# A graph-attention layer on one core: 138 instead of 120 groups of edges counted, and eight more looked up, weighed and gathered last

## The chip, the cores and the metric

The kernel runs on one core of one Trainium2 chip. The metric is device microseconds of one execution, the median of three runs. The profile is of one more execution, taken by the hardware profiler. PE is TensorE, DVE VectorE, ACT ScalarE, POOL GpSimd and SP SyncE.

## The reference

A layer of graph attention over 12,500 nodes with 64 features and 400,000 edges with 64 features, a residual and a layernorm. The edges are sorted by destination, and destinations are drawn so that low node numbers have far more edges than high ones.

```python
h_src, h_dst = x[src], x[dst]
e = leaky_relu(concat([h_src, h_dst, edge]) @ W_attn + b_attn)[:, 0]
m = concat([h_src, edge]) @ W_ne
ex = exp(e - segment_max(e, dst)[dst])
alpha = ex / segment_sum(ex, dst)[dst]
z = segment_sum(alpha[:, None] * m, dst)
out = layernorm(x + relu(concat([x, z]) @ W_out))
```

So each edge needs its source's row of `x` twice: its dot product with a part of `W_attn` for the score, and the row itself, weighed by `alpha`, for the sum.

## The kernel before

**Groups.** 512 edges make a group (128 partitions by 4 edges), and there are 782 groups, the last of them a quarter full. A group takes one of two ways.

*Gathered groups* (662, from group 120 on). Four indirect DMAs per group, issued from GpSimd (L335), fetch the source rows with their score's part from a table in HBM into a buffer `zx` of four groups (a "part"); there are nine such buffers (`ZB`). SyncE's queue loads the edge features beside them. `scores` (L366 to L388, VectorE) makes a part's scores; L377 is the instruction that waits for the gathered rows. `softmax` (L664 on) then treats a whole batch at once, in four legs, between which the ends of its rows go through a one-partition line and back by DMA (L599, L605). It begins with a transpose (L694). `weights` (L791) spreads alpha over the destinations' slots, `products` (L808, in the last two batches L812) are the matmuls, and `add_in` (L827) adds them to `acc`.

*Dense groups* (the first 120, whose few destinations have thousands of edges each). They need no gather. First they are *looked up*: ScalarE turns the low seven bits of the source numbers into ones and zeros (`look_turn`, L427 and L428), TensorE multiplies by the table of scores (`look_products`, L438), VectorE picks by the high bits (`look_scores`, L463 to L469), and `look_rows` (L448 on) adds the edges' share. Then whole rounds of dense groups join a batch's softmax in its spare rows. Then they are *counted* (`dense_counts`, L477 to L493): ScalarE makes one tile per edge place of ones at the pair (high bits, destination's place), in buffers called `big`, VectorE makes `lows`, ones at the low bits times alpha (L480), and TensorE multiplies the two into a table source by destination, which `dense_sum` (L503, and L506 for the sixth and seventh destination of a group) adds into `counts`. At the end of a chunk of groups `counts` is multiplied by `x` (L562) and set to zero (L575).

**The order of the work** is written out by hand. Every engine runs its instructions in the order of the code. There are 43 batches: 39 of 16 groups, then 10, 10, 12 and 6. In batch `k` the code first issues the gathers (of parts one to three, the fourth a little later, so GpSimd runs ahead), then does the parts' scores, and between these and the softmax's legs a few dense groups: the next ones to be looked up and the next ones to be counted. `alike` says how many: at most four (before group 84) or three (from there), and never across a round's begin, a change in the number of destinations (`NODS`) or, for counts, a chunk's end. A round is free for counting once its look-ups are done and it has joined a softmax. Counts end in batch 38. Blocks of four times 128 nodes are finished (`finish0` to `finish3`: projection, residual, layernorm, output) as soon as no later edge can reach them; block 0, which holds the dense groups' destinations, in three steps in one of the late batches.

**The tail.** After the last batch's softmax come its weights, its products (L812), the additions (L827), and the last two blocks' matmuls (L1042) and layernorm (L1071 to L1090).

**The head** packs the sources' low bits into rows for the look-ups (`low_rows`), loads the dense groups' lists round by round (`dense_list`, L230) and works out their places.

Of the kernel before, what the change touches and what calls it, by code (L numbers as in the profile page):

```python
# [9 lines left out]
F32 = mybir.dt.float32  # L10
I32 = mybir.dt.int32
# [4 lines left out]
P = 128  # L16
# [11 lines left out]
BIG = 6  # L28
# [7 lines left out]
ROUNDS = (12, 12, 12, 12, 12, 12, 12, 12, 12, 12)  # L36
DB = len(ROUNDS)
EACHS = ((84, 4), (120, 3))
EACH = max(n for _, n in EACHS)
# [19 lines left out]
def sorted_path(ctx, tc, x, dst, idx, edge, w_ne, w_attn, b_attn, w_out, out, flag):  # L59
# [24 lines left out]
    ones_row = const.tile([1, P], F32, name="ones_row")  # L84
    nc.vector.memset(ones_row, 1.0)
# [24 lines left out]
    assert HC * ND == P and HC * D <= 512 and sum(chunk_sizes) == DG == NODS[-1][0]  # L110
# [4 lines left out]
    def each_of(g):  # L115
        return next(n for upto, n in EACHS if g < upto)

# [7 lines left out]
    edges_ = sorted({*begins, *(upto for upto, _ in NODS), *(upto for upto, _ in EACHS)})  # L125
    spans = list(zip(edges_, edges_[1:]))
    DN = DBL * P

# [37 lines left out]
    places = const.tile([P, NB * NOD], I16, name="places")  # L166
    nc.gpsimd.iota(places, pattern=[[1, NB * NOD]], base=0, channel_multiplier=0,
                   allow_small_or_imprecise_dtypes=True)
    s_src = const.tile([P, NB], F32, name="s_src")
    low, place = (const.tile([P, T, DG], F32, name=n) for n in ("low", "place"))  # L170
# [11 lines left out]
    rel = const.tile([1, DG], I32, name="rel")  # L182
# [40 lines left out]
    _, sixth, seventh, probe = cut(pps, 2 * P, NB, NB, 8)  # L223
    more_nodes, w_dst, w_src = (sixth, seventh), sixth[:, 0:D], seventh[:, 0:D]
# [18 lines left out]
    def dense_places(srcs, fit):  # L243

        assert max(n for _, n in NODS) <= FIT + len(more_nodes)
# [7 lines left out]
        nc.scalar.activation(low, parted[1], AF.Copy)  # L253
# [7 lines left out]
        nc.vector.tensor_tensor(place, high, wide(fit[:, 1]), op=OP.mult)  # L261
        nc.vector.tensor_tensor(place, place, slot_, op=OP.subtract)
        for a, b in spans:
            if nodes_of(a) > FIT:
# [24 lines left out]
    def slots_of(k):  # L289

        g0, G = starts[k], sizes[k]
        drel = chunks.tile([P, T, BG], F32, name="drel", bufs=3)
# [69 lines left out]
    def scores(g0, n, zx, drel, b0, plain):  # L362
# [6 lines left out]
        pr = feats.tile([P, SG, T, D], F32, name="pr", bufs=1)  # L369
# [37 lines left out]
    def look_loads(g0, n):  # L407

        many = nodes_of(g0)
        wrow = tiny.tile([P, EACH, NOD], F32, name="wrow_d", bufs=1)[:, :, 0:many]  # L410
        nc.sync.dma_start(out=wrow[:, 0:n], in_=wins[0][g0:g0 + n, 0:many].unsqueeze(0).to_broadcast([P, n, many]))
        return dense_edges(g0, n, "ed", True), wrow
# [28 lines left out]
    def look_rows(g0, n, loads):  # L441
# [4 lines left out]
        pr = feats.tile([P, SG, T, D], F32, name="pr", bufs=1)  # L446
# [12 lines left out]
    def look_scores(g, found):  # L459

        pr = feats.tile([P, SG, T, D], F32, name="pr", bufs=1)
# [9 lines left out]
    def dense_counts(g):  # L471
# [14 lines left out]
        for j in range(nodes_of(g) - FIT):  # L486
            at = wide + j * NB
            hi = big().rearrange("l p t -> l (p t)")[:, 0:T * NB].rearrange("l (t h) -> l t h", t=T)
            for t in range(T):
                nc.scalar.activation(hi[:, t], places[:, at:at + NB], AF.Square, bias=place[:, t, g:g + 1])  # L490
            nc.scalar.activation(hi, hi, AF.Relu, scale=-1.0, bias=1.0)
            for t in range(T):
                nc.tensor.matmul(more_nodes[j], lows[t], hi[:, t], start=(t == 0), stop=(t == T - 1), skip_group_check=True)  # L493
        return g, to

    def dense_sum(g, to):
# [7 lines left out]
        for j in range(nodes_of(g) - FIT):  # L504
            at = counts[:, :, ds(vs[0] + FIT + j, 1)]
            nc.vector.tensor_tensor(at, at, more_nodes[j].unsqueeze(2), op=OP.add)  # L506
# [9 lines left out]
    def dense_weights(g0, n):  # L516

        many = nodes_of(g0)
        w = tiny.tile([P, T * EACH * NOD], F32, name="wd", bufs=1)[:, 0:T * EACH * many]
# [6 lines left out]
        return w  # L526

# [38 lines left out]
    def node_pick(g0, pairs):  # L566

        pr = feats.tile([P, SG, T, D], F32, name="pr", bufs=1)
# [5 lines left out]
        if g0 + chunk_sizes[-1] < DG:  # L574
            nc.vector.memset(counts, 0.0)  # L575
# [55 lines left out]
    def between(k):  # L631
# [13 lines left out]
        mask = rows.tile([P, 2, P], F32, name="mask", bufs=2)  # L645
        nc.scalar.activation(mask, pen, AF.Relu, bias=1.0)
        return step, same, pen, mask

    def at_ends(step, same, pen, mask):
# [6 lines left out]
    def lines_of(step, same, pen, mask):  # L656
# [4 lines left out]
        return step, same, pen, mask, rw  # L661

    def softmax(k, about, carry, d=None, carry_d=None):
# [8 lines left out]
        step, same, pen, mask = about[0:4]  # L672
# [29 lines left out]
        to_lines(ends_of, bnd)  # L702
        yield
        in_lines()
        rw = about[4]
# [158 lines left out]
    ids = pre.tile([DG, P, 2 * T], I32, name="ids", bufs=1)  # L864
    nc.sync.dma_start(out=ids, in_=idx[0:DG])
# [10 lines left out]
    with before:  # L876
# [23 lines left out]
        with tc.manual_schedule(engines={EngineType.DVE, EngineType.Pool, EngineType.Activation, EngineType.PE, EngineType.SP}):  # L900
# [27 lines left out]
            nc.vector.tensor_copy(edge_both, pwt[:, 2, 0:D])  # L928
            d0f = pre.tile([1, NG], F32, name="d0f", bufs=1)
# [7 lines left out]
            relf = pre.tile([1, DG], F32, name="relf", bufs=1)  # L937
# [5 lines left out]
            room = pre.tile([1, DG], F32, name="room", bufs=1)  # L943
            for a, b in spans:
                nc.vector.memset(room[:, a:b], float(ND - nodes_of(a)))
            over_ = pre.tile([1, DG], F32, name="over_", bufs=1)
# [13 lines left out]
            parted_row = pre.tile([DG, P, T], I32, name="parted_row", bufs=1)  # L960
# [867 lines left out]
```

## Time and profile before

| | |
|---|---|
| median of 3 runs | 3384.53 us (3383.27 to 3386.39) |
| the profiled execution | 3384.66 us |
| its span, first to last instruction | 3382.9 us |
| TensorE matmul busy | 2128.5 us (63%) |
| VectorE busy | 2141.7 us (63%) |
| ScalarE busy | 1227.2 us (36%) |
| GpSimd busy | 2513.2 us (74%) |
| DMA from HBM | 241.09 MB |

Busy time counts instructions that work, and not the time an engine spends on registers, semaphores or issuing. A group of rows in the profile is "line, engine, operation, out<-in, xcount | busy us, mean ns of one | idle time before them and what ended it". In a list of waits the columns are total, times and longest. In a timeline they are start, duration, engine, line, and in brackets the idle time before and what ended it. A line number is one of the kernel before.

### The profile page before, as it was taken

How to read it: one execution, taken by the hardware profiler on the slowest of the kernel's cores; microseconds unless marked ns; L12 is line 12 of the kernel's file. 1: busy time of each engine (PE TensorE's matmuls, PEld its weight loads, DVE VectorE, ACT ScalarE, POOL GpSimd, SP SyncE). 2: the span in 40 equal slices, each digit the busy share in tenths (PEclk: the TensorE clock that was granted, in tenths of full speed). 3: DMA queues.
4: the chain of work that ended last, by engine and by line, in shares of the span. 5: the costliest groups of instructions: out<-in, count | busy, mean ns of one | idle time of the engine just before them, and what ended most of it. 6: DMA issues, size and time to landing. Idle time of an engine off the chain costs nothing. (4 is left out here: it accounts for less than half of the span.)

```text
span 3382.9 us, 38194 instructions
## 1 busy us (share of the span) xinstructions
PE 2128.5 (63%) x9584; PEld 1795.6 (53%) x9584; DVE 2141.7 (63%) x5517; ACT 1227.2 (36%) x2835; POOL 2513.2 (74%) x2676
## 2 busy tenths in 40 slices
PE   0254445666666677586778777655767675776663
PEld 0244445566555566465656555554556564554562
DVE  5654455666666676666676666665677775666665
ACT  0111123333343344434444343333454343544321
POOL 6777777777777777777777777777777777777772
PEclk9999985555555666666667676656766676766655
DMA  9433343343444444434434333333343433342331
GB/s 130 86 68 68 67 74 74 74 78 74 74 78 79 83 76 85 87 72 79 86 76 75 72 74 73 68 72 71 73 80 73 79 74 56 71 77 52 66 64 27
DMA packets 815285, 250.94 MB, mean 74 GB/s; under 512 B 736090, under 2 KB 772633, under 8 KB 815058
## 3 DMA queue, kind: packets, MB, share of 16 engines
q1 hardware_dynamic: 688364, 159.40, 24.0%
q0 software_dynamic: 84960, 88.33, 15.5%
q10 hardware_dynamic: 41734, 0.67, 0.7%
q8 instruction: 83, 1.36, 0.2%
q14 instruction: 144, 1.18, 0.1%
HBM read 241.09 MB, written 6.79 MB: 73 GB/s over the span
## 5 line engine op out<-in xcount | busy, mean ns | idle before, releaser
L335 POOL DMA_INDIRECT zx<-table,srcs x2584 | 2442.8, 945 | 787.3 <-issue 719.0
L808 PE MATMUL pg<-w,zx 128*128 128x16 f32 (+9 forms) x5152 | 994.5, 362 | 171.7 <-DMA zx<-table,srcs 98.0
L808 PEld LDWEIGHTS pg<-w,zx 128*128 128x128 f32 x5152 | 974.2, 294 | 189.3 <-issue 98.1
L485 PE MATMUL pg<-big,lows 128*128 128x490 f32 (+3 forms) x960 | 510.6, 694 | 356.5 <-DVE lows L480 248.1
L485 PEld LDWEIGHTS pg<-big,lows 128*128 128x128 f32 x960 | 250.2, 276 | 570.3 <-issue 316.7
L438 PE MATMUL pg<-s_src,big 128*128 128x98 f32 x960 | 258.2, 448 | 317.5 <-DVE pr L465 177.4
L438 PEld LDWEIGHTS pg<-s_src,big 128*128 128x128 f32 x960 | 234.8, 329 | 321.0 <-issue 179.3
L377 DVE TENSOR_TENSOR fixed<-fixed,zx 128x16 f32<-128x16 f32 (+3 forms) x172 | 31.7, 184 | 485.3 <-DMA zx<-table,srcs 481.4
L477 ACT ACTIVATE big<-places,place 128x490 f32<-128x490 int16 (+3 forms) x480 | 294.6, 614 | 60.3 <-PE pg L438 31.3
L372 DVE TENSOR_REDUCE fixed<-pr 128x16 f32<-128x1024 f32 (+3 forms) x172 | 204.2, 1187 | 129.3 <-ACT fixed L368 119.5
L478 ACT ACTIVATE big<-big 128x490 f32<-128x490 f32 (+3 forms) x480 | 257.1, 536 | 15.3
L696 ACT ACTIVATE soft<-turned 128x128 f32<-128x128 f32 x43 | 16.7, 388 | 540.8 <-DVE turned L694 540.8
L368 ACT ACTIVATE fixed<-wrow 128x96 f32<-128x96 f32 (+11 forms) x172 | 45.5, 265 | 456.6 <-DVE lows L480 141.3
L370 DVE TENSOR_TENSOR pr<-zx,lines 128x1024 f32<-128x1024 f32 (+3 forms) x172 | 202.0, 1175 | 6.4 <-DMA zx<-in_edge_dram 6.3
L827 DVE TENSOR_TENSOR acc<-acc,pg 128x16 f32 (+9 forms) x662 | 122.9, 186 | 71.6 <-issue 21.1
L480 DVE TENSOR_SCALAR lows<-fixed,low,kept 128x128 f32<-128x128 f32 x480 | 163.5, 401 | 1.0 <-PE pg L485 0.9
L562 PE MATMUL pg<-xall,counts 128*128 128x256 f32 x600 | 161.0, 436 | 0.1
L562 PEld LDWEIGHTS pg<-xall,counts 128*128 128x128 f32 x600 | 132.2, 224 | 26.9 <-issue 4.0
L427 ACT ACTIVATE big<-low_of,p_col 128x512 f32<-128x512 bf16 x120 | 86.4, 720 | 164.5 <-DMA low_of<-low_rows 134.1
L803 PE MATMUL pg<-zx,ident 1*1 1x32 f32 (+3 forms) x344 | 42.0, 207 | 163.2 <-issue 132.5
L803 PEld LDWEIGHTS pg<-zx,ident 1*1 1x1 f32 x344 | 14.2, 76 | 202.8 <-issue 158.9
L379 DVE TENSOR_TENSOR hot<-fixed,drel 128x384 bf16<-128x384 f32 (+11 forms) x172 | 109.2, 635 | 14.1 <-DMA counts<-sdflat,d0p 8.2
(379 smaller groups left out, 2545.6 us busy)
## 6 DMA issues: line engine op xcount, KB each, us to landing
zx<-in_edge_dram SPq DMA_DIRECT2D x661, 128.0 KB
zx<-table,srcs POOLq DMA_INDIRECT x2584
low_of<-low_rows SPq DMA_DIRECT2D x120, 128.0 KB
ep<-in_edge_dram SPq DMA_DIRECT2D x120, 128.0 KB
ed<-in_edge_dram SPq DMA_DIRECT2D x21, 512.0 KB
ed<-in_edge_dram SPq DMA_DIRECT2D x12, 384.0 KB
table<-xall SPq DMA_DIRECT2D x7, 455.0 KB
out_dram<-yo SPq DMA_DIRECT2D x24, 128.0 KB
```

What stands on the lines that cost most here:

```text
L335: nc.gpsimd.indirect_dma_start(out=zx[0:r, g, t, 1:EW] if plain else zx[0:r, g, t, 0:EW], out_offset=None, in_=x[:, :] if plain else table ...
L370: nc.vector.tensor_tensor(pr[0:r, 0:n], ze[0:r, 0:n], w_edge[0:r].unsqueeze(1).to_broadcast([r, n, T, D]), op=OP.mult)
L372: nc.vector.tensor_reduce(ysum[0:r, 0:n], pr[0:r, 0:n], axis=AX.X, op=OP.add)
L379: nc.vector.tensor_tensor(hot[0:r, 0:n], slots[0:r, 0:Sk].unsqueeze(1).unsqueeze(1).to_broadcast([r, n, T, Sk]), drel[0:r, :, b:b + n].rea ...
L438: nc.tensor.matmul(found[:, t, :], hot[:, :, t], s_src, start=True, stop=True)
L477: nc.scalar.activation(hi, places[:, 0:wide], AF.Square, bias=place[:, t, g:g + 1])
L478: nc.scalar.activation(hi, hi, AF.Relu, scale=-1.0, bias=1.0)
L480: nc.vector.tensor_scalar(lows[t], count_, low[:, t, g:g + 1], kept[:, t, kept_at(g):kept_at(g) + 1], op0=OP.is_equal, op1=OP.mult)
L485: nc.tensor.matmul(to, lows[t], highs[t], start=(t == 0), stop=(t == T - 1))
L562: nc.tensor.matmul(pairs[0:m * ND, 0:m * D], counts[:, h0:h0 + m, :].rearrange("l h n -> l (h n)"), xall[:, h0:h0 + m, 1:EW], start=(h0 == ...
L808: nc.tensor.matmul(pg[:, g, :], zx[:, g, t, 1:EW + D], w[:, g, t, :], start=(t == 0), stop=(t == T - 1)).ins
L827: nc.vector.tensor_tensor(ag, ag, pg[:, g, :], op=OP.add)
```

## The change

*More dense groups.* `ROUNDS` now sums to 146, in 15 uneven rounds of 5 to 15 groups instead of ten of 12. 138 of them are looked up and counted. The last eight (`LATER`), groups 138 to 145, are looked up and weighed with the last round, but not counted: behind the last batch's gathers GpSimd gathers their rows too, and behind the last batch's products TensorE multiplies them by weights known by then (`late_weights`, `late_products`, `late_sums`). Gathered groups are 636 and, last, these eight. There are 41 batches: 38 of 16 groups, then 10, 10 and 8.

*More per batch.* Up to five look-ups per batch throughout, up to five counts (before group 94) and then four; the third of five counts stands between the third and the fourth part's scores. Chunks are cut anew: 17 instead of 12. A look-up left over behind the softmax's legs is done right after it.

*Less room.* `big` has five buffers instead of six. A count's sixth and seventh destinations are made together, two edge places at a time.

*Moved.* `mask` is made within the softmax. Block 0 is finished at the very end, since the late groups reach it. The head loads lists in 15 pieces and packs the low bits in two halves, since 146 groups are more than 128 partitions.

```diff
-BIG = 6
+BIG = 5
-ROUNDS = (12, 12, 12, 12, 12, 12, 12, 12, 12, 12)
+ROUNDS = (10, 9, 10, 5, 15, 14, 9, 9, 8, 12, 9, 10, 7, 11, 8)
-EACHS = ((84, 4), (120, 3))
+LOOKS = ((146, 5),)
+EACHS = ((94, 5), (138, 4))
-CHUNKS = ((36, 1), (12, 2), (8, 3), (6, 6))
-NODS = ((16, 2), (36, 3), (60, 4), (87, 5), (108, 6), (120, 7))
+CHUNKS = ((34, 1), (15, 1), (10, 1), (9, 3), (8, 1), (4, 1), (7, 1), (3, 1), (6, 1), (4, 1), (6, 1), (3, 1), (4, 2), (3, 1))
+NODS = ((14, 2), (34, 3), (63, 4), (89, 5), (108, 6), (138, 7), (146, 8))
+LATER = 8
-    ENDS = ((3, 3, 2, 2), (3, 3, 2, 2), (3, 3, 3, 3), (2, 2, 1, 1))
+    ENDS = ((3, 3, 2, 2), (3, 3, 2, 2), (3, 2, 2, 1))
     DG = sum(ROUNDS)
+    DC = DG - LATER
...
-        for j in range(nodes_of(g) - FIT):
-            at = wide + j * NB
-            hi = big().rearrange("l p t -> l (p t)")[:, 0:T * NB].rearrange("l (t h) -> l t h", t=T)
-            for t in range(T):
-                nc.scalar.activation(hi[:, t], places[:, at:at + NB], AF.Square, bias=place[:, t, g:g + 1])
+        more = max(0, nodes_of(g) - FIT) * NB
+        for t0 in range(0, T if more else 0, 512 // max(more, P)):
+            ts = range(t0, min(t0 + 512 // max(more, P), T))
+            hi = big().rearrange("l p t -> l (p t)")[:, 0:len(ts) * more].rearrange("l (t h) -> l t h", h=more)
+            for i, t in enumerate(ts):
+                nc.scalar.activation(hi[:, i], places[:, wide:wide + more], AF.Square, bias=place[:, t, g:g + 1])
             nc.scalar.activation(hi, hi, AF.Relu, scale=-1.0, bias=1.0)
...
+    def late_products(g0, n, zx, w):
+        many = nodes_of(DC)
+        pg = psum.tile([P, SG, P], F32, name="pg", bufs=4)[:, 0:n, 0:many]
+        for g in range(n):
+            for t in range(T):
+                nc.tensor.matmul(pg[:, g, :], zx[:, g, t, 1:EW + D], w[:, g0 - DC + g, t, :],
+                                 start=(t == 0), stop=(t == T - 1))
+        return g0, n, pg
...
+                        if final:
+                            late_parts = []
+                            for g in range(DC, DG, SG):
+                                m = min(SG, DG - g)
+                                edges(g, m)
+                                late_parts.append((g, m, gather(g, m, late_list, DC, False)))
+                            late_w = late_weights()
...
+                    if i == 3 and len(batch_counts) > 4:
+                        if opened:
+                            opened = node_pick(*opened)
+                            picked_ = True
+                        while open_counts:
+                            dense_sum(*open_counts.pop(0))
+                        open_counts.append(dense_counts(batch_counts[2]))
                     hot = scores(g0, n, tiles[i], drel, b0, k == 0)
...
+            late_parts = [late_products(*part, late_w) for part in late_parts]
             add_up()
             for part in fronts:
                 behind_front(*part)
+            for part in late_parts:
+                late_sums(*part)
+            fronts.append(finish2(*x0))
         for part in fronts:
             finish3(*part, more=False)
```

How this moves instructions, at three places. First GpSimd's queue, the gathers of the whole run. `zx` are the row buffers, `counts` is lent to seven small gathers of the head (L880). Before:

```order
L335 DMA zx<-in_x_dram,srcs 128x64 x32
L880 DMA counts<-sdflat,d0p 128x48 x2
L335 DMA zx<-in_x_dram,srcs 128x64 x32
L880 DMA counts<-sdflat,d0p 128x48 x5
L335 DMA zx<-table,srcs 128x65 x2580
L335 DMA zx<-table,srcs 32x65 x4
```

The same queue of the changed kernel, where the lines are L341 and L927:

```order
L341 DMA zx<-in_x_dram,srcs 128x64 x32
L927 DMA counts<-sdflat,d0p 128x48 x2
L341 DMA zx<-in_x_dram,srcs 128x64 x32
L927 DMA counts<-sdflat,d0p 128x48 x5
L341 DMA zx<-table,srcs 128x65 x2476
L341 DMA zx<-table,srcs 32x65 x4
L341 DMA zx<-table,srcs 128x65 x32
```

There are 104 gathers fewer ahead of the quarter group that ends the last batch (32x65), and 32 behind it.

Second, ScalarE in a softmax with dense work, between the DMA of the second leg's row ends and the copy that takes them up, here the end of that piece in the softmax of batch 30. `lines` and `strip` are the line's tiles, `dens` the sums of the rows. Before:

```order
L477 ACTIVATE big_17961<-places_110,place_114 128x490
L478 ACTIVATE big_17961<-big_17961 128x490
L490 ACTIVATE big_17971<-places_110,place_114 128x98 x4
L491 ACTIVATE big_17971<-big_17971 128x392
L599 ACTIVATE lines_149<-strip_83 1x256
L605 ACTIVATE strip_83<-dens_78 1x2x32x4
L602 DMA ini_84<-strip_83 128x1x2
L477 ACTIVATE big_18006<-places_110,place_114 128x490
```

And in the changed kernel's batch 30, whose group has two destinations beyond five instead of one:

```order
L486 ACTIVATE big_19522<-places_108,place_112 128x490
L487 ACTIVATE big_19522<-big_19522 128x490
L501 ACTIVATE big_19532<-places_108,place_112 128x196 x2
L502 ACTIVATE big_19532<-big_19532 128x392
L501 ACTIVATE big_19538<-places_108,place_112 128x196 x2
L502 ACTIVATE big_19538<-big_19538 128x392
L643 ACTIVATE lines_147<-strip_81 1x256
L649 ACTIVATE strip_81<-dens_76 1x2x32x4
L646 DMA ini_82<-strip_81 128x1x2
L436 ACTIVATE big_19573<-low_of_19500,p_col_106 128x512
L437 ACTIVATE big_19573<-big_19573 128x512
L486 ACTIVATE big_19581<-places_108,place_112 128x490
```

A count's last part is longer, and a look-up's turn (L436, L437) stands in the leg behind the copy.

Third, TensorE's end. `pps` holds the last two blocks, `wd` the late groups' weights, `accd` and `acce` the dense destinations' sums. Before:

```order
L812 MATMUL pg<-w,zx 64x48 x16
L803 MATMUL pg<-zx,ident 1x8
L812 MATMUL pg<-w,zx 64x48 x8
L803 MATMUL pg<-zx,ident 1x8
L812 MATMUL pg<-w,zx 64x48 x8
L1042 MATMUL pps<-both,acc 128x64 x6
```

And in the changed kernel:

```order
L847 MATMUL pg<-zx,ident 1x8
L856 MATMUL pg<-w,zx 64x48 x8
L559 MATMUL pg<-wd,zx 128x8 x32
L1093 MATMUL pps<-both,acc 128x64 x6
L1074 MATMUL pg<-twice,xtt 128x2x64 x2
L1103 MATMUL pg<-both,accd 128x64
L1105 MATMUL pg<-edge_both,acce 128x64
```

The late groups' 32 matmuls stand ahead of the last two blocks' (L1093), and block 0's two and eight behind them.

More of the change, by code (lines that the diff above doesn't have):

```diff
@@ L116, in each_of, with look_of @@
         return next(n for upto, n in EACHS if g < upto)
+    def look_of(g):
+        return next(n for upto, n in LOOKS if g < upto)
     def round_of(g):
@@ L503, in dense_sum @@
         nc.vector.tensor_tensor(at, at, to.rearrange("p (h n) -> p h n", n=n), op=OP.add)
-        for j in range(nodes_of(g) - FIT):
-            at = counts[:, :, ds(vs[0] + FIT + j, 1)]
-            nc.vector.tensor_tensor(at, at, more_nodes[j].unsqueeze(2), op=OP.add)
+        more = nodes_of(g) - FIT
+        if more > 0:
+            at = counts[:, :, ds(vs[0] + FIT, more)]
+            nc.vector.tensor_tensor(at, at, more_nodes[g % 2][:, 0:more * NB].rearrange("p (j h) -> p h j", h=NB), op=OP.add)
     def dense_keep(g, fac):
@@ L566, in node_pick @@
     def node_pick(g0, pairs):
[L568 removed]
+        pr = feats.tile([P, EACH, T, D], F32, name="pr", bufs=1)
         mine = pr[:, 0]
@@ L644, in between, with at_ends @@
         nc.scalar.activation(pen[:, 1, :], far[:, 1:P + 1], AF.Identity, bias=nfar)
[L645 to L649, printed above, removed]
+        return step, same, pen
+    def at_ends(step, same, pen):
         outer_ = rows.tile([P, 2], F32, name="outer_", bufs=2)
@@ L654, in at_ends, with lines_of @@
         to_lines(pens_of, outer_)
-    def lines_of(step, same, pen, mask):
+    def lines_of(step, same, pen):
         rw = tiny.tile([1, 4, P], F32, name="rw", bufs=1)
@@ L671, in softmax @@
         assert d is None or G == BS
-        step, same, pen, mask = about[0:4]
+        step, same, pen = about[0:3]
         flat_m = mrow.rearrange("o k i -> o (k i)")
@@ L863, in sorted_path @@
     lists[1] = listed(1)
-    ids = pre.tile([DG, P, 2 * T], I32, name="ids", bufs=1)
-    nc.sync.dma_start(out=ids, in_=idx[0:DG])
+    halves = [(a, min(a + P, DG)) for a in range(0, DG, P)]
+    ids = []
+    for a, b in halves:
+        ids.append(pre.tile([P, P, 2 * T], I32, name=f"ids{a}", bufs=1)[0:b - a])
+        nc.sync.dma_start(out=ids[-1], in_=idx[a:b])
     nc.sync.dma_start(out=meet, in_=dst[DG * GE - 1:DG * GE + 1].unsqueeze(0))
@@ L1149, in sorted_path, with alike @@
         loads = rows_again = None
-        def alike(todo, ends_=chunk_ends):
+        def alike(todo, ends_=chunk_ends, each=each_of):
             n = 0
-            while n < min(each_of(todo[0]) if todo else 0, len(todo)) and not (n and todo[n] in edges_) and not (n and todo[n] in ends_):
+            while n < min(each(todo[0]) if todo else 0, len(todo)) and not (n and todo[n] in edges_) and not (n and todo[n] in ends_):
                 n += 1
@@ L1189, in sorted_path @@
                     columns_of(k + 2)
+                elif not final:
+                    late_list = chunks.tile([P, BS, 2 * T], I32, name="srcs", bufs=3)
+                    nc.sync.dma_start(out=late_list[:, 0:LATER], in_=idx[DC:DG].rearrange("g p c -> p g c"))
                 if k:
                     joined = resting
-                    batch_looks = alike(looks, ())
+                    batch_looks = alike(looks, (), look_of)
                     batch_counts = alike(counting)
@@ L1287, in dense_step @@
                         raised()
-                    if n == 0 and opened:
+                    if n == 0 and opened and not picked_:
                         opened = node_pick(*opened)
@@ L1384, in sorted_path @@
                     ready[k + 2] = slots_of(k + 2)
+            assert resolved_at is not None and not (looks or counting or edges_of or summed)
+            late_parts = [late_products(*part, late_w) for part in late_parts]
             add_up()
```

128 lines of the change are left out of this document (75 added, 53 removed).

## The prediction

> **What bounds the kernel now.** I read the page first, for the engine with the largest share.
>
> ```profile
> span 3382.9 us, 38194 instructions
> ...
> PE 2128.5 (63%) x9584; PEld 1795.6 (53%) x9584; DVE 2141.7 (63%) x5517; ACT 1227.2 (36%) x2835; POOL 2513.2 (74%) x2676
> ...
> L335 POOL DMA_INDIRECT zx<-table,srcs x2584 | 2442.8, 945 | 787.3 <-issue 719.0
> ```
>
> GpSimd is busy for 74%, but nearly all of its idle time is "issue", time in which it waited for nothing that the profile shows. So its true share is higher. The timeline of its queue near the end says how high:
>
> ```profile
> 3299.73 0.94 POOL L335 DMA_INDIRECT zx<-table,srcs  x1 [0.30 <-issue]
> ...
> 3312.21 0.94 POOL L335 DMA_INDIRECT zx<-table,srcs  x1 [0.30 <-issue]
> ...
> 3329.46 0.87 POOL L335 DMA_INDIRECT zx<-table,srcs  x1 [0.30 <-issue]
> ```
>
> Ten gathers lie between the first two starts: 12.48 us, or 1.248 us each, and the last one ends at 3330.3. There are 662 gathered groups of four gathers, 2648 in all, and 2648 x 1.248 = 3305 us, all but 25 us of the time to 3330.3. GpSimd is the bound from the head to that point. Next I asked whether the step depends on what the other engines do, with the table of stages for one light batch and one dense batch:
>
> ```profile
> 346.60:426.50 79.90, 36.59 (x168) 35.41 (x168) 38.62 (x103) 13.95 (x36) 60.41 (x65) 1.00 0.37 69
> 2425.90:2506.00 80.10, 54.61 (x246) 44.38 (x246) 57.87 (x138) 36.62 (x81) 60.60 (x65) 0.61 0.40 76
> ```
>
> The columns are length, then busy time and count of PE, PEld, DVE, ACT and POOL. A batch of 16 groups takes 80 us in both, although VectorE's work goes from 38.6 to 57.9. So work on the other engines is free as long as a batch keeps under 80 us. How much room is left is read from VectorE's waits for gathered rows, in three stages: 13 batches from 426.5 to 1466.4, 8 from there to 2106.1, and the last 10 dense ones, 2346.5 to 3145.7 (its first line, and the line under it, are of this last stage).
>
> ```profile
> DVE fixed L377 <- DMA zx<-table,srcs: 203.7, 26, 11.2
> ...
> DVE fixed L377 <- DMA zx<-table,srcs: 79.1, 13, 9.7
> ...
> DVE fixed L377 <- DMA zx<-table,srcs: 61.3, 10, 11.0
> DVE dens L740 <- ACT lines L599: 48.6, 10, 7.3
> ```
>
> The room is 15.7, 9.9 and 6.1 us per batch. In the last stage VectorE also loses 4.9 us per batch to ScalarE, whose copy for the softmax stands behind counting work.
>
> **The gathers.** The 26 groups more that need no gather are 18 groups less to gather altogether, and 8 more whose gathers move behind the last softmax's. GpSimd reaches the end of the last batch's gathers after 2544 instead of 2648: 104 x 1.248 = **129.8 us** earlier, at 3200.5. The 32 late gathers follow until 3240.4. This holds if GpSimd is never made to wait.
>
> **The added dense work.** Look-ups per batch go from four or three to five, counts from four or three to five or four. Prices of VectorE's rows:
>
> ```profile
> L463 DVE TENSOR_TENSOR pr<-fixed,high 128x392 f32<-128x392 f32 x120 | 65.2, 543 | 0.4
> L465 DVE TENSOR_TENSOR pr<-pr,pg 128x392 f32<-128x392 f32 x120 | 67.5, 562 | 22.4 <-PE pg L438 13.8
> L467 DVE TENSOR_REDUCE picked<-pr 128x4 f32<-128x392 f32 x120 | 67.3, 561 | 4.1
> L448 DVE TENSOR_TENSOR pr<-ed,lines 128x1024 f32<-128x1024 f32 (+1 forms) x33 | 36.7, 1112 | 0.0
> L480 DVE TENSOR_SCALAR lows<-fixed,low,kept 128x128 f32<-128x128 f32 x480 | 163.5, 401 | 1.0 <-PE pg L485 0.9
> L503 DVE TENSOR_TENSOR counts<-counts,pg 128x490 f32 (+3 forms) x120 | 69.4, 578 | 42.5 <-PE pg L485 24.3 <-issue 14.8 <-DVE counts L503 0.9
> L575 DVE MEMSET counts<- 128x3136 f32 x11 | 29.4, 2672 | 6.6 <-issue 6.6
> ```
>
> Divided by 120 groups, a look-up costs 0.54 + 0.56 + 0.56 + 0.31 = 1.97 us and a count 1.36 + 0.58 = 1.94; a chunk's memset costs 2.67. Replaying the rule of `alike` on both sets of tables, I count work by batch. First stage, batches 5 to 17: 62 look-ups against 52, 58 counts against 52, so 10 x 1.97 + 6 x 1.94 = 31 us on 203.7 of room. Batches 18 to 25: one look-up and three counts more, 7.8 on 79.1. Both fit. The last ten dense batches (28 to 37, against 29 to 38): 26 look-ups against 15, 33 counts against 30, eight chunks against five: 21.7 + 5.8 + 8.0 = 35.5 us, and with the small rows left out some 45, on 61.3. On the mean this fits, with under 2 us per batch to spare. But the load is uneven (a batch with five look-ups and four counts beside one with one and two), and ScalarE's queue lengthens in the softmax's way by a look-up's turn:
>
> ```profile
> L427 ACT ACTIVATE big<-low_of,p_col 128x512 f32<-128x512 bf16 x120 | 86.4, 720 | 164.5 <-DMA low_of<-low_rows 134.1
> L428 ACT ACTIVATE big<-big 128x512 f32<-128x512 f32 x120 | 75.6, 630 | 3.8
> ```
>
> That is 1.35 us, in at most two legs of seven batches: 0 to 19 us. Room is 61.3 - 45 - (0 to 19), so +16 to -3 in sum, and what uneven batches overrun is carried along. GpSimd does not feel it: nine row buffers are two batches and a quarter, so VectorE may lag by some 40 us before a gather waits for its buffer. But a lag left at the end is paid in full. I take **+10 us**, from 0 to 25.
>
> **The last batches.** From one softmax's transpose to the next:
>
> ```profile
> 3145.73 0.32 DVE L694 STREAM_TRANSPOSE turned<-soft 128x128 f32<-128x128 f32 x1
> ...
> 3205.97 0.24 DVE L694 STREAM_TRANSPOSE turned<-soft 128x128 f32<-128x128 f32 x1
> ...
> 3255.75 0.24 DVE L694 STREAM_TRANSPOSE turned<-soft 128x128 f32<-128x128 f32 x1
> ...
> 3306.21 0.24 DVE L694 STREAM_TRANSPOSE turned<-soft 128x128 f32<-128x128 f32 x1
> ...
> 3343.23 0.24 DVE L694 STREAM_TRANSPOSE turned<-soft 128x128 f32<-128x128 f32 x1
> ```
>
> Batches of 10, 10, 12 and 6 groups take 60.2, 49.8, 50.5 and 37.0, in sum 197.5 against 189.7 of gathers: VectorE falls 7.8 behind, and the last transpose comes 12.9 after the last gather's end. Now they are 10, 10 and 8. The first has a chunk and a joined round behind it (+4: 64.2), the second 49.8, the third 41.5 (a third of the way from 37.0 to 50.5): 155.5 against 112 x 1.248 = 139.8, which is 15.7 behind: **+7.9 us**. The last transpose is at 3200.5 + 12.9 + 7.9 + 10 = 3231.3.
>
> **The tail.** From the last transpose on:
>
> ```profile
> 3362.74 1.95 PE L812 MATMUL pg<-w,zx 128*64 128x48 f32 x32 [9.87 <-DVE w L791]
> ...
> 3369.56 2.82 PE L1042 MATMUL pps<-both,acc 128*128 128x64 f32 x12 [0.56 <-DVE acc L827]
> ...
> 3372.42 0.43 DVE L1071 SCALAR_TENSOR_TENSOR pps<-pps,xall 128x256 f32<-128x256 f32 x1 [2.67 <-PE pps L1042]
> ...
> 3375.32 0.42 DVE L1090 TENSOR_TENSOR yo<-yo,var 128x256 f32<-128x256 f32 x1
> ...
> 3376.51 0.29 DVE L1090 TENSOR_TENSOR yo<-yo,var 128x128 f32<-128x128 f32 x1
> ```
>
> From transpose to end it was 39.7. TensorE starts the last products 19.5 after it, so at 3250.8; the late rows were all requested by 3240.4, ten earlier, so the late gathers cost nothing. If VectorE had no lag at all, the late matmuls, behind eight groups' products, would still find them landed. What they bring is on TensorE, in order, ahead of the last blocks' matmuls (L1042's kind). Two more groups in the last batch: one row above, 1.95. Then 32 late matmuls, each two records:
>
> ```profile
> 162.75 7.00 PE L808 MATMUL pg<-w,zx 128*128 128x12 f32 x32
> ...
> 2969.08 3.77 PE L808 MATMUL pg<-w,zx 128*128 128x44 f32 x32
> ```
>
> Sixteen took 7.00 in one place and 3.77 in another, so 32 take 14.0 or 7.5. The stretch around 162 was back to back from 155.4 on and still slow, and its tiles are as narrow, so I take 14.0. In the Trainium skill, "TensorE: Matmul & The Clock Gate", Part 1, sustained work of some 3.4 us releases the clock: by it the late matmuls would be nearer 7.5 and the sum 6.5 lower. The row at 162.75 speaks against it here. Behind that stands block 0, which used to be done long before: VectorE's eight late additions (some 0.2 each, partly between the others' steps, +0.1 beyond the old 4.4 of both fronts), eight matmuls at 2.82 / 6 = 0.47, 3.8 us, and its own six VectorE steps in a row, 3.3 (from 3372.42 to 3375.74, the first front's). Fronts' steps lie under none of it, since VectorE's additions must end before block 0's matmuls. Sum: 2.0 + 14.0 + 0.1 + 3.8 + 3.3 = **+23.2 us**.
>
> **The head.** Fifteen list loads instead of ten, and a second half of the packed rows:
>
> ```profile
> 71.61 12.06 SPq L230 DMA_DIRECT2D dense_srcs<-in_idx_dram  x10
> ...
> 102.73 0.36 DVE L379 TENSOR_TENSOR hot<-fixed,drel 128x192 bf16<-128x192 f32 x1 [8.21 <-DMA counts<-sdflat,d0p]
> ```
>
> Five loads more are 6.0 us on SyncE's queue, and VectorE has 8.2 idle there, behind gathers. Should that cover go, the room in the first batches takes it. Nothing. Masks made later, the third count moved between parts two and three, and the look-up left over behind the softmax are work that is only moved; the room of its batch hides it.
>
> **The sum.** The profiled execution took 3384.66 (span 3382.9 and 1.8 around it), 0.1 above the median of 3384.53. 3384.66 - 129.8 + 10 + 7.9 + 23.2 = **3296.0 us**.
>
> **Rivals.**
>
> *VectorE's chain becomes the bound in the last dense stage.* For it: 6.1 us of room per batch, and five buffers of `big` instead of six. Against: the mean still fits. If the added work costs as much again in waits, 90 against 61.3, a lag of 29 grows, and with the uneven batches 40 to 60: 3326 to 3346, say 3336. It decides from 7.5 us added per batch.
>
> *A memset locks gathers out.* One gather was stretched beside one:
>
> ```profile
> 161.76 3.93 POOL L335 DMA_INDIRECT zx<-table,srcs  x1 [0.30 <-issue]
> 162.07 2.67 DVE L1240 MEMSET counts<- 128x3136 f32 x1 [0.63 <-issue]
> ...
> 1869.76 0.94 POOL L335 DMA_INDIRECT zx<-table,srcs  x1 [0.30 <-issue]
> 1869.92 2.67 DVE L575 MEMSET counts<- 128x3136 f32 x1 [0.60 <-issue]
> ```
>
> The second pair shows the same memset beside a gather of usual length. The change has 16 chunk memsets where 11 were. If each cost a gather 3.93 - 0.94 = 2.99, that is 48 us: 3344. The Trainium skill has this rule: "SBUF — State Buffer", "SBUF: two separate sides", says that VectorE in a two-port mode holds the port that GpSimd needs to write descriptors. The trace agrees once and disagrees at 1869.
>
> *Slower than before: the ring of five.* A count fills four buffers of `big`; with one less, ScalarE, in order, may have to wait for TensorE to drain the count before, and the softmax's copies stand behind it.
>
> ```profile
> L485 PE MATMUL pg<-big,lows 128*128 128x490 f32 (+3 forms) x960 | 510.6, 694 | 356.5 <-DVE lows L480 248.1
> ```
>
> Draining one count is 510.6 / 120 = 4.3 us, and 4.5 counts make 19 us per batch. A batch now needs 80 less its room, 64.3, 70.1 and 73.9 in the three stages; with 2.4, 1.0 and 4.5 added and 19 on top it needs 85.7, 90.1 and 97.4, over 80 by 5.7, 10.1 and 17.4, in 13, 8 and 13 batches 381 us: 3667. Above 82.6 us per dense batch (88.6 / 34 more than 80) the kernel is slower than before; at half of the wait, 107 us over, it is 3393. Against: ScalarE hardly waits for TensorE today.
>
> *No change.* The gathers saved come back as waits of the same size, 2.6 us per dense batch, by the same ring at a little under half price: 3385.
>
> **How the numbers follow.** Forecast 0.68, last stage bound 0.20, memsets 0.03, ring of five 0.06, no change 0.03. The forecast's own spread is from no lag and a fast clock, 3296 - 10 - 6.5, less some 10 for the last batches' estimate, to a lag of 25 and a little more: 3268 to 3320. To leave out at most 2 in 10 the range takes in the lower half of the next case: **3268 to 3332**. Within 0.2% (6.8 us, about what a measurement of this kernel can tell) 0.03, faster 0.91, slower 0.06.
>
> **What would show it.** Right: 2576 gathers at steps of 1.248, the last batch's gathers done near 3200, waits at L377 (its line now) above zero in most dense batches, late gathers over before the last products, block 0 last. Wrong: gather steps above 1.25 in dense batches, no wait for rows over several batches, a last transpose more than 45 us behind its gathers, or late matmuls that take 7 us.

## The result, and the profile after

The change makes the kernel a little faster, by a quarter of what was forecast.

| | before | after |
|---|---|---|
| median of 4 runs | 3384.49 us (3383.27 to 3386.39) | 3362.68 us (3353.35 to 3367.30) |
| ratio, 95% interval | | 0.9932 (0.9910 to 0.9953) |
| the profiled execution | 3384.66 us | 3367.30 us |

Four more runs (the kernel before with four buffers twice, and the late products ahead twice) were made at times when the kernel before itself took 4543 to 4569 us; their ratios to it, 1.045, 1.034 and twice 1.036, are compared with nothing here, and both kernels were run again later beside a kernel before of 3385 us.

The forecast was 3296.0, from 3268 to 3332. In the profiled execution, the longest of the four, 71.3 us have to be accounted for. The page of the changed kernel, span, busy times and the gathers' row:

```profile
span 3365.6 us, 39853 instructions
...
PE 2339.4 (70%) x10140; PEld 1942.5 (58%) x10140; DVE 2236.4 (66%) x5760; ACT 1372.8 (41%) x3060; POOL 2445.5 (73%) x2606
...
L341 POOL DMA_INDIRECT zx<-table,srcs x2512 | 2375.0, 945 | 836.9 <-issue 695.2
```

One gather takes 945 ns as before. GpSimd's idle time that is not "issue" is larger: 836.9 - 695.2 = 141.7, where it was 787.3 - 719.0 = 68.3. Its timeline shows where, in the last third of the kernel:

```profile
2640.15 0.94 POOL L341 DMA_INDIRECT zx<-table,srcs  x1 [0.30 <-issue]
2656.88 0.94 POOL L341 DMA_INDIRECT zx<-table,srcs  x1 [15.78 <-PE pg L852]
...
3174.05 0.94 POOL L341 DMA_INDIRECT zx<-table,srcs  x1 [0.30 <-issue]
3194.91 0.94 POOL L341 DMA_INDIRECT zx<-table,srcs  x1 [19.92 <-PE pg L852]
...
3310.68 0.94 POOL L341 DMA_INDIRECT zx<-table,srcs  x1 [0.30 <-issue]
```

A gather now waits for a row buffer that the products (L852) have not yet read. In all, by the list of GpSimd's waits, it is 68.4 us in 12 waits:

```profile
POOL zx L341 <- PE pg L852: 68.4, 12, 19.9
```

That is nearly all of the 71.3 that are missing. GpSimd stands because VectorE is late, and how late (its *lag*) is read where the last three batches begin: how much later than in the kernel before the transpose of the same batch starts (L694, now L736). In the kernel before it is at 3066:

```profile
3065.78 0.32 DVE L694 STREAM_TRANSPOSE turned<-soft 128x128 f32<-128x128 f32 x1
```

```profile
3144.97 0.32 DVE L736 STREAM_TRANSPOSE turned<-soft 128x128 f32<-128x128 f32 x1
...
3304.36 0.24 DVE L736 STREAM_TRANSPOSE turned<-soft 128x128 f32<-128x128 f32 x1
```

Then come that transpose and the last one in the changed kernel. VectorE is 79.2 us behind. The last three batches then take 159.4 (forecast 155.5), and from the last transpose to the span's end it is 61.2 (forecast 62.9). So one term is wrong, the lag: 10 us forecast, 79 measured.

The waits that grew. First the kernel before, then the changed one (VectorE's wait for gathered rows; ScalarE's count tile that waits for a look-up's product; VectorE's `step`, for the next batch's softmax, that waits for ScalarE's copy `far`):

```profile
DVE fixed L377 <- DMA zx<-table,srcs: 481.4, 65, 12.4
...
DVE step L639 <- ACT far L635: 32.4, 14, 6.5
...
ACT big L477 <- PE pg L438: 31.3, 9, 10.9
```

```profile
ACT big L486 <- PE pg L447: 209.5, 26, 14.3
DVE step L683 <- ACT far L679: 194.5, 33, 14.3
...
DVE fixed L383 <- DMA zx<-table,srcs: 150.9, 27, 12.4
```

One such place, in the batch that begins at 1226, in ScalarE's, TensorE's and VectorE's timelines:

```profile
1265.24 0.70 ACT L436 ACTIVATE big<-low_of,p_col 128x512 f32<-128x512 bf16 x1
...
1278.01 0.72 ACT L436 ACTIVATE big<-low_of,p_col 128x512 f32<-128x512 bf16 x1
...
1281.45 0.60 ACT L486 ACTIVATE big<-places,place 128x392 f32<-128x392 int16 x1
...
1296.30 0.62 ACT L486 ACTIVATE big<-places,place 128x392 f32<-128x392 int16 x1 [13.68 <-PE pg L447]
...
1297.59 0.29 ACT L679 ACTIVATE far<-edges_of 128x130 f32<-128x130 int32 x1
```

```profile
1279.46 12.54 PE L606 MATMUL pg<-xall,counts 128*128 128x256 f32 x50
1291.92 2.40 PE L590 MATMUL pg<-wd,ep 128*128 128x8 f32 x20
1294.18 2.08 PE L447 MATMUL pg<-s_src,big 128*128 128x98 f32 x8
```

```profile
1297.92 0.29 DVE L683 CUSTOM_DVE_ANT_0 step<-far 128x129 f32<-128x129 f32 x1 [11.94 <-ACT far L679]
```

ScalarE has filled two buffers for look-ups, at 1265.24 and 1278.01, and three of four for a count, and that is all five. The fourth count tile has to wait until the first look-up's buffer is read, but that product stands in TensorE's order behind 12.54 us of chunk products. ScalarE stands for 13.68 us, `far` stands behind it, and VectorE loses 11.94.

*Theory 1:* the ring of five `big` buffers is the cause. *Theory 2:* the added look-ups and counts are more than a batch has room for, whatever the ring.

### The profile page after: what moved, and what is told of

Same layout as the page of the kernel before. It is cut to its first block, busy times and chain, and to the rows that moved or that the text cites. A ratio compares the mean times of both kernels' runs of the same rounds, so it can differ in the third digit from the quotient of the medians.

```text
span 3365.6 us, 39853 instructions
## 1 busy us (share of the span) xinstructions
PE 2339.4 (70%) x10140; PEld 1942.5 (58%) x10140; DVE 2236.4 (66%) x5760; ACT 1372.8 (41%) x3060; POOL 2445.5 (73%) x2606
## 5 line engine op out<-in xcount | busy, mean ns | idle before, releaser
L341 POOL DMA_INDIRECT zx<-table,srcs x2512 | 2375.0, 945 | 836.9 <-issue 695.2
L852 PE MATMUL pg<-w,zx 128*128 128x20 f32 (+9 forms) x4944 | 976.0, 369 | 182.1 <-DMA zx<-table,srcs 100.6
L852 PEld LDWEIGHTS pg<-w,zx 128*128 128x128 f32 x4944 | 956.2, 300 | 199.3 <-issue 100.8
L494 PE MATMUL pg<-big,lows 128*128 128x490 f32 (+3 forms) x1104 | 586.9, 690 | 325.6 <-DVE lows L489 265.8
L486 ACT ACTIVATE big<-places,place 128x490 f32<-128x490 int16 (+3 forms) x552 | 344.9, 625 | 325.3 <-PE pg L447 209.5
L378 DVE TENSOR_REDUCE fixed<-pr 128x16 f32<-128x1024 f32 (+2 forms) x164 | 196.0, 1195 | 110.0 <-ACT fixed L374 96.4
L606 PE MATMUL pg<-xall,counts 128*128 128x256 f32 (+1 forms) x850 | 223.7, 430 | 0.4 <-DVE yo L1126 0.4
L606 PEld LDWEIGHTS pg<-xall,counts 128*128 128x128 f32 (+1 forms) x850 | 184.2, 221 | 37.0 <-issue 5.6
L376 DVE TENSOR_TENSOR pr<-zx,lines 128x1024 f32<-128x1024 f32 (+2 forms) x164 | 194.0, 1183 | 1.9 <-DMA zx<-in_edge_dram 1.4
L436 ACT ACTIVATE big<-low_of,p_col 128x512 f32<-128x512 bf16 x146 | 105.1, 720 | 154.2 <-DMA low_of<-low_rows 98.5
L871 DVE TENSOR_TENSOR acc<-acc,pg 128x20 f32 (+9 forms) x636 | 118.6, 187 | 69.2 <-issue 19.4
L514 DVE TENSOR_TENSOR counts<-counts,pg 128x490 f32 (+3 forms) x138 | 80.9, 586 | 72.5 <-PE pg L494 51.9
L385 DVE TENSOR_TENSOR hot<-fixed,drel 128x576 bf16<-128x576 f32 (+8 forms) x164 | 106.7, 650 | 6.1 <-issue 0.3
```

The costliest lines, as they stand in the source:

```text
L341: nc.gpsimd.indirect_dma_start(out=zx[0:r, g, t, 1:EW] if plain else zx[0:r, g, t, 0:EW], out_offset=None, in_=x[:, :] if plain else table ...
L376: nc.vector.tensor_tensor(pr[0:r, 0:n], ze[0:r, 0:n], w_edge[0:r].unsqueeze(1).to_broadcast([r, n, T, D]), op=OP.mult)
L378: nc.vector.tensor_reduce(ysum[0:r, 0:n], pr[0:r, 0:n], axis=AX.X, op=OP.add)
L385: nc.vector.tensor_tensor(hot[0:r, 0:n], slots[0:r, 0:Sk].unsqueeze(1).unsqueeze(1).to_broadcast([r, n, T, Sk]), drel[0:r, :, b:b + n].rea ...
L486: nc.scalar.activation(hi, places[:, 0:wide], AF.Square, bias=place[:, t, g:g + 1])
L494: nc.tensor.matmul(to, lows[t], highs[t], start=(t == 0), stop=(t == T - 1))
```

## The experiments

**The ring alone, back at six.** The sixth buffer's room comes from two things that matter only in the last batch.

```diff
-BIG = 5
+BIG = 6
...
-xtt = work.tile([P, NBC // 2, P], F32, name="xtt", bufs=2)
+xtt = work.tile([P, NBC // 2, P], F32, name="xtt", bufs=1)
...
-w = tiny.tile([P, WD], F32, name="wd", bufs=1)[:, 0:LATER * T * many]
+w = big().rearrange("l p t -> l (p t)")[:, 0:LATER * T * many]
```

> The changed kernel with its ring of large one-hot buffers back at six (room for the sixth from two small things of the last batch: one transposed-block buffer in place of two, and the late weights put into one of the six). Theory 1 (with five buffers ScalarE's fourth count tile of a batch needs the look-up's buffer, whose product stands in TensorE's queue behind 12.5 us of chunk products; far and the softmax's copies stand behind it on ScalarE, and VectorE's step waits for far): the waits of the count tiles for TensorE's look-up product go from 209 us to under 60 us, the wait of step for far from 194 us to under 60 us, and the time to 3290 to 3320 us. Theory 2 (the added look-up and count of each batch are themselves more than the room, whatever the ring): the waits shift, the time stays at 3350 us or more.

Measured: 3310.38 us, ratio to the kernel before 0.9786 (0.9770 to 0.9803). The list of waits:

```profile
DVE fixed L383 <- DMA zx<-table,srcs: 229.0, 40, 12.3
...
DVE step L683 <- ACT far L679: 72.1, 16, 13.0
ACT big L501 <- PE pg L447: 65.1, 9, 12.7
...
ACT big L486 <- PE pg L447: 40.6, 12, 9.2
```

52 us of the 67 missing ones were the ring's. `step` still waits 72.1 us, where theory 1 had expected under 60. What is left of the count's wait for the look-up's product is now mostly at L501, the further tile for groups with six and more destinations. With it a batch asks for a seventh buffer; seven were not run.

**The same ring in the kernel before.**

```diff
-BIG = 6
+BIG = 5
```

> The kernel before with five large buffers in place of six, nothing else. Theory 1: in the batches with chunk products the fourth count tile waits about 12 us for the look-up's product, as in the changed kernel, and step waits for far; of the 12 batches concerned those with 10 to 16 us of room hide most of it, and the time is 3385 to 3420 us with the wait of step for far over 100 us. Theory 2: no such waits of size, and 3384 us within 5.

Measured: 3383.92 us, ratio 1.0001 (0.9991 to 1.0010). Theory 1 had the waits right and the time wrong, theory 2 the time right and the waits wrong:

```profile
DVE fixed L377 <- DMA zx<-table,srcs: 392.3, 54, 12.4
...
DVE step L639 <- ACT far L635: 117.6, 32, 16.2
```

The wait for `far` grew by 85 us (the count tiles' wait for the look-up's product from 31.3 to 129.7), and the wait for gathered rows shrank by 89. The ring's price was there, but the batches' room paid it.

**Four buffers, in both kernels.** `BIG = 4`, nothing else. In the changed kernel:

> The changed kernel with four large buffers in place of five, nothing else. Theory 1 (the ring): a batch asks for two look-up buffers, four count buffers and, from six nodes on, one or two more. Six to five cost 52 us once the room was gone; one more buffer less makes the third count tile wait as well: 3400 us or more, the wait of step for far above 300 us. Theory 2 (the five-buffer ring was no more than a shift of waits that another engine would have had anyway): within 10 us of the changed kernel's 3362.

Measured: 3408.71 us, ratio 1.0073 (1.0057 to 1.0090). In the kernel before:

> The kernel before with four large buffers in place of six, on a chip on which the kernel before takes 3384 us: 3384 to 3395 us with the wait for gathers near 300 us if a buffer's price is paid out of room batch by batch; 3420 us or more with GpSimd standing still for 30 us or more if the price is flat.

Measured: 3385.40 us, ratio 1.0002 (0.9992 to 1.0011), with

```profile
DVE fixed L377 <- DMA zx<-table,srcs: 325.5, 52, 12.4
...
DVE step L639 <- ACT far L635: 151.8, 34, 15.7
```

and no wait of GpSimd for products over 0.3 us.

| buffers | kernel before | changed kernel |
|---|---|---|
| 6 | 3384.5 | 3310.4 |
| 5 | 3383.9 | 3362.7 |
| 4 | 3385.4 | 3408.7 |

A buffer less costs 46 to 52 us in the changed kernel, where there is no room, and nothing in the kernel before, where there is. (`step`'s wait in the changed kernel came to 211.3 with four, not to the 300 that was expected; what grew was the count tiles' wait for the counts' own products, from 103.8 to 201.4.)

**Chunk products behind the look-up's, with five buffers and with six.**

```diff
 if i == 0:
-    if chunk_of is not None:
-        opened = node_products(chunk_of)
     if edges_of or batch_looks or chunk_of is not None:
         shared = spare()
...
     seen.append((batch_looks[0], look_products(turns.pop(0), shared)))
+if i == 1 and chunk_of is not None:
+    opened = node_products(chunk_of)
```

> The changed kernel with five buffers, and the 25 chunk products put into TensorE's queue behind the first look-up's four products instead of ahead of them. Theory 1: the look-up's buffer comes free some 12 us earlier, the count tile's wait for the look-up's product falls under 80 us in all (from 209), step's wait for far under 80 us (from 194), time 3295 to 3330 us. Theory 2: the order of TensorE's products doesn't matter, 3350 us or more. A third outcome, that the chunk products now delay the count's own products and sums, would show as VectorE waiting for TensorE at the count's sums, and give back part of it.

Measured with five: 3360.02 us (3355.13 to 3362.26), ratio 0.9925 (0.9908 to 0.9941), which can't be told from the changed kernel. The waits only changed their names:

```profile
DVE step L683 <- ACT far L679: 159.4, 30, 14.8
ACT big L501 <- PE pg L494: 141.9, 28, 12.6
...
ACT big L486 <- PE pg L494: 133.4, 24, 15.6
...
ACT big L486 <- PE pg L447: 100.1, 22, 8.9
```

ScalarE's wait for the look-up's product halves (209.5 to 100.1), and that for counts' products grows by about as much (L486 from 103.8 to 133.4, L501 from 61.1 to 141.9).

> Six buffers, and the chunk products behind the first look-up's products. With six buffers the waits left over are the ones of the further one-hot tile of groups with six and more nodes (63 us for the look-up's product between 2032 and 2938 us). If that product's place behind 12.5 us of chunk products is their cause, step's wait for far falls from 72 us to under 30 us and the time from 3310 to 3295 or less. If only the number of buffers counts, as with five, the wait moves to the count's own products and the time stays at 3305 to 3315 us.

Measured with six: 3295.94 us (3293.27 to 3296.79), ratio 0.9734 (0.9718 to 0.9751). GpSimd's wait, the lag, and the last batch's last gather (its last start before the late ones):

```profile
POOL zx L341 <- PE pg L852: 2.8, 6, 1.3
```

```profile
3074.52 0.32 DVE L736 STREAM_TRANSPOSE turned<-soft 128x128 f32<-128x128 f32 x1
```

```profile
3199.73 0.86 POOL L341 DMA_INDIRECT zx<-table,srcs  x1 [0.30 <-issue]
...
3239.60 0.94 POOL L341 DMA_INDIRECT zx<-table,srcs  x1 [0.31 <-issue]
```

The lag is 8.7 us (10 forecast), the batches' gathers end at 3200 and the late ones at 3240, as forecast. `step`'s wait for `far` fell to 43.8 us, where under 30 was expected. With two buffer settings and two orders, the order is worth nothing at five and 14 us at six. Theory 2 falls: the same look-ups and counts fit, at the gathers' pace.

**`far` ahead of the counts.** The lines that make `far`, `step`, `same` and `pen` for the next batch are put ahead of `dense_counts`.

```diff
+if i == (0 if final else 1):
+    if more:
+        as_floats(k + 2, lists[k + 2])
+    if k + 1 < len(sizes):
+        after = between(k + 1)
 if k and i in (1, 2):
     for g in batch_counts[i - 1:i] if i == 1 or len(batch_counts) > 3 else ():
         open_counts.append(dense_counts(g))
```

> The changed kernel with five buffers, and far, step, same and pen of the next batch written ahead of the batch's first count instead of behind it. ScalarE still waits for the look-up's product, but far no longer stands behind that wait. Theory 1: the wait of step for far goes from 194 us to under 40 us; if that wait is what VectorE loses, the time is 3295 to 3330 us; if the wait only moves to the next thing that ScalarE is late with (the count's one-hot tiles, the softmax's boundary copies), 3340 to 3362 us. Theory 2: 3350 us or more with the waits moved.

> Six buffers, and far, step, same and pen ahead of the batch's first count. Step's wait for far goes (72 us to under 25 us). If what VectorE loses in the batches from 2032 us on is that wait, 3290 to 3300 us; if ScalarE stays late and VectorE then waits for the next batch's score copies, as with five buffers (where that wait grew to 94 us in this stretch), 3303 to 3312 us.

Measured with five: 3353.16 us (3347.99 to 3356.31), 0.9906 (0.9889 to 0.9922), ranges that overlap with the changed kernel's. With six: 3326.97 us, 0.9833 (0.9817 to 0.9849), 17 us *more* than without the step; neither expectation (3290 to 3300, or 3303 to 3312) had that. With six buffers, the line that took the place of `step`'s:

```profile
DVE fixed L378 <- ACT fixed L374: 204.5, 60, 27.3
```

It was 87.1 without the step. So `far` was only the place where VectorE met a late ScalarE; moved out of the way, VectorE meets it at the next part's score copies.

**The late part alone.** The changed kernel's code with the tables of before, six buffers, 128 groups looked up, 120 counted, eight late.

```diff
-ROUNDS = (10, 9, 10, 5, 15, 14, 9, 9, 8, 12, 9, 10, 7, 11, 8)
+ROUNDS = (12, 12, 12, 12, 12, 12, 12, 12, 12, 12, 8)
...
-LOOKS = ((146, 5),)
-EACHS = ((94, 5), (138, 4))
+LOOKS = ((84, 4), (128, 3))
+EACHS = ((84, 4), (120, 3))
...
```

> The late part alone: the changed kernel's code with the tables of before (rounds of 12, four and then three groups a batch, twelve chunks) and six large buffers, but 128 groups looked up and weighed, 120 counted, the last eight gathered behind everything; last batches of 10, 11 and 9 groups. By the prediction's terms: 32 gathers fewer before the last softmax are 39.9 us off, the late gathers and their matmuls and sums are 23.2 us on, a last batch of nine groups in place of six about 8 us on: 3376 us, 3366 to 3384. If the late part hides its matmuls better than that, 3360 or less; if it is what spoils the changed kernel, 3385 or more.

Measured: 3361.61 us, ratio 0.9934 (0.9917 to 0.9951). The late part alone, with six buffers, gives as much as the whole change gave with five. It is 14 us better than the middle of what was expected, and those are the last batches and the tail: the last transpose comes some 13 us behind the end of the last of the batches' gathers, where 12.9 and about 8 more were expected,

```profile
3289.65 0.86 POOL L341 DMA_INDIRECT zx<-table,srcs  x1 [0.30 <-issue]
```

```profile
3303.66 0.24 DVE L736 STREAM_TRANSPOSE turned<-soft 128x128 f32<-128x128 f32 x1
```

and from there to the end it is 55.6, not 62.9, with late products of 10.3 us, where the changed kernel's took 13.8.

**The late products ahead.** On top of six buffers and the chunk products behind, the late products and sums stand ahead of the last batch's products.

```diff
 if final:
+    for part in [late_products(*part, late_w) for part in late_parts]:
+        late_sums(*part)
     for i, (g0, n, zx, w) in enumerate(lasts):
...
-late_parts = [late_products(*part, late_w) for part in late_parts]
...
-for part in late_parts:
-    late_sums(*part)
```

> The late products and sums ahead of the last batch's (six buffers, chunk products behind the look-up's), on a chip on which the kernel before takes 3384 us: 3280 to 3286 us if the 12.7 us of late products and 1.8 us of late sums stand on the path to the end, 3290 us or more if something else sets the end.

Measured: 3289.47 us (3286.30 to 3291.90), ratio 0.9717 (0.9701 to 0.9733), the fastest of all. It is 6.5 us faster than without the step, between the two expectations and less than half of the 14.5 us that were moved away. TensorE's timeline without the step:

```profile
3262.29 12.75 PE L559 MATMUL pg<-big,zx 128*128 128x8 f32 x64
3274.89 2.80 PE L1093 MATMUL pps<-both,acc 128*128 128x64 f32 x12
```

and with it:

```profile
3243.51 13.82 PE L559 MATMUL pg<-big,zx 128*128 128x8 f32 x64 [0.24 <-DVE some L1046]
...
3267.97 2.82 PE L1093 MATMUL pps<-both,acc 128*128 128x64 f32 x12 [3.95 <-DVE acc L871]
```

The late products are out of the way, and the last blocks' matmuls now wait 3.95 us for VectorE's additions of the last batch, which lay under the late products before. The last batch's products also start 1.6 us later than without the step (3257.42 against 3255.83), straight behind the late ones.

## Why the prediction was wrong, point by point

- **The gathers, right.** 2576 gathers, 1.249 us from one to the next on the median. The 129.8 us were there to be had: with six buffers and the chunk products behind, the batches' gathers end at 3200, where the forecast put them. In the changed kernel they end 71 us later, at 3271.7, since the term's condition ("if GpSimd is never made to wait") didn't hold.
- **The added dense work, the step that failed.** It set added work (45 us of VectorE's rows, 0 to 19 of ScalarE's) against VectorE's room of 61.3 and took +10 from 0 to 25 for unevenness. The sum of rows was good: in the changed kernel's ten batches, 2300.4 to 3145.0, VectorE is busy for 578.9 us, where it was 533.4, so 45.5 more. And it was enough: at six buffers with the chunk products behind, the lag was 8.7. But the room was needed a second time, for what the ring makes ScalarE wait. That price was dealt with apart, as a rival that either isn't there ("ScalarE hardly waits for TensorE today") or drains a whole count, 19 us a batch, and got 0.06. It was neither: 52 us, which over the 23 batches between 1226 and 3145 is 2.3 us each.
- **The earlier stages, put at nothing.** "Both fit" was said of batches 5 to 25, since the added rows (31 and 7.8 us) are far below the room (203.7 and 79.1). The lag says otherwise. It is the start of the same batch's transpose less that in the kernel before, whose starts are in the first column; the other columns are versions of the changed kernel:

| before, us | four buffers | five | six | six, chunk products behind |
|---|---|---|---|---|
| 1226 | 0.8 | -0.1 | -1.6 | -0.6 |
| 1306 | 17.4 | 13.0 | 1.7 | 4.2 |
| 1706 | 22.9 | 11.1 | -1.6 | -0.6 |
| 2266 | 61.2 | 34.2 | 10.1 | 2.2 |
| 2906 | 120.3 | 83.2 | 32.0 | 17.3 |
| 3066 | 117.5 | 79.2 | 20.1 | 8.7 |

With five buffers 34 of the 79 us were there by 2266, ahead of the ten batches for which the prediction allowed a lag, and 13 came from the one batch shown above. Room added up over a stage did not tell what a single long wait costs.

- **"ScalarE hardly waits today"** was read with six buffers, exactly what two look-ups and one count's four tiles ask for. In the kernel before, one buffer less makes 85 us of wait for `far` appear, and the reading could not show that, as it could not show that it costs nothing there.
- **The rival "no change"** named the same ring, at 2.6 us in each of 34 dense batches, 88.6 in all, and got 0.03. 66.7 were missing, 52 of them the ring's. Its 3385 is 22 us off, the nearest of the rivals, though the gathers saved were not lost in full.
- **The rival of VectorE's chain** (0.20) had the right place, with the five buffers among its reasons, and a lag of 40 to 60 where it was 79: its 3336 is 27 us off. It took "no wait for gathered rows over several batches" for its sign. That sign came up (no such wait from 1226 to 3145), but it tells little: with six buffers and the chunk products behind, VectorE waited 9.7 us for rows in the 985 us from 2089 to 3074, and the kernel still ran at the gathers' pace, for the row buffers carried the lag. The other sign, a last transpose more than 45 us behind its gathers, did not come up: it was 32.7 (3304.36 against 3271.7), since GpSimd itself had been held.
- **How much lag the row buffers carry** was put at some 40 us. GpSimd first stood at 2640, when VectorE was 60 us behind the kernel before:

```profile
2586.41 0.32 DVE L694 STREAM_TRANSPOSE turned<-soft 128x128 f32<-128x128 f32 x1
```

```profile
2646.87 0.32 DVE L736 STREAM_TRANSPOSE turned<-soft 128x128 f32<-128x128 f32 x1
```

  With six buffers it stood for 12.4 us from 3124 on, at a lag of some 20, in the last batches, whose parts have one to three groups: nine buffers hold less there.

- **The memsets, rightly left out.** 16 chunk memsets, and one gather still 945 ns on the mean. Only the gather beside the head's memset is stretched by more than 1 us, as in the kernel before: 4.1 us at 163.7. The rule of the Trainium skill, "SBUF — State Buffer", "SBUF: two separate sides", speaks of a two-port mode, and no run here shows whether these memsets use one; so the rival's 48 us are not borne out, and the rule itself is not tested.
- **The last batches and the tail, right, with some luck.** 159.4 against 155.5, and 61.2 against 62.9. The late matmuls took 13.8 us against 14.0. But the row at 162.75, taken for the slow clock, lies in a stretch (155.4 to 170) for which the table of stages gives a granted clock of 1.00, so it does not show that the clock made it slow; and with six buffers and the chunk products behind, the same late matmuls took 12.8 us, with the late part alone 10.3. That the former kernel's 3295.9 meets the forecast to 0.1 is luck in part: its last three batches took 161.4 and its end 58.6, which nearly cancel. That the late matmuls lie on the path in full was half wrong: taken away, they give back 6.5, for VectorE's last additions lay under them.

What stays open: why `far` ahead of the counts costs 17 us with six buffers was traced to ScalarE's score copies, but not tried further; and whether a seventh buffer would take away the rest of the waits, for which there was no room.

## What to carry to other kernels

When a change takes a buffer away and spends the slack of the same stages, price both against the same slack: the buffer's wait may cost nothing before and all of its length after. Count how many buffers the work asks for between two drains (here two for look-ups, four for count tiles, and a seventh from six destinations on) before reading "hardly waits" as room to spare. An engine's wait that is moved away by reordering may only turn up at that engine's next product, so look at who is late, not at which wait is longest.

## What the runs showed of the hardware that was not expected

The granted clock fell in the middle of uninterrupted work. In the kernel with six buffers and `far` first, TensorE shows no gap from 3286.6 on; the table of stages (length, busy times of PE, PEld, DVE, ACT, POOL, then the granted clock):

```profile
3288.00:3290.00 2.00, 2.00 (x40) 1.85 (x38) 0.98 (x5) 0.43 (x3) 0.00 (x0) 0.50 0.01 0
3290.00:3292.00 2.00, 2.00 (x60) 1.87 (x58) 1.16 (x6) 0.00 (x0) 0.00 (x0) 0.94 0.32 66
...
3296.00:3298.00 2.00, 2.00 (x16) 2.00 (x16) 0.16 (x1) 0.00 (x0) 0.00 (x0) 0.76 0.00 0
3298.00:3300.00 2.00, 2.00 (x11) 2.00 (x11) 0.00 (x0) 0.00 (x0) 0.00 (x0) 0.50 0.00 0
```

The clock rose some 3.6 us into the work and fell again some 7 us later, while the narrow late matmuls ran back to back. In the changed kernel the same stretch stayed at the slow clock throughout:

```profile
3332.40:3339.00 6.60, 6.60 (x33) 6.58 (x32) 0.41 (x2) 0.00 (x0) 0.00 (x0) 0.50 0.01 2
3339.00:3346.00 7.00, 7.00 (x34) 7.00 (x34) 0.16 (x1) 0.00 (x0) 0.00 (x0) 0.50 0.00 0
```

By the Trainium skill, "TensorE: Matmul & The Clock Gate", Part 1, some 3.4 us of sustained work release the clock. The first kernel's rise agrees; its fall, and the changed kernel's 13.6 us of busy TensorE at 0.50, do not. The same 32 late matmuls took 9.9 us in the first kernel and 13.8 in the changed one. "Busy" is the profile's, whose matmul ends are modelled, so it does not say how full the array was. What decides the clock was not tried.
